# Another front for the first group of an RWKV-6 block: loads on two queues, norm and mixing shared between engines, and new due times

## The chip, the cores and the metric

The kernel runs on one core of one Trainium2 chip. The metric is device time in microseconds (us) of one launch. The engines carry these names: PE is TensorE (PEld its weight loads), DVE is VectorE, ACT is ScalarE, POOL is GpSimd, SP is SyncE, which here only issues DMAs. "SPq" and "ACTq" are the DMA-issuing sequencers of SP and ACT.

## The reference

One RWKV-6 block in f32 on x of 32 rows (batch) × 128 tokens × 512 channels; 32 heads of 16 channels. Cut to what matters:

```python
xn = ln(x, ln1_w, ln1_b); sx = shift(xn, prev) - xn       # shift: the token before, prev ahead of the first
xxx = tanh((xn + sx * maa_x) @ maa_w1)                    # 5 vectors of 32
xxx = matmul(xxx, maa_w2)                                 # 5 x 512
x5 = xn + sx * (maa_stack + xxx)                          # the five "mixings"
w = exp(-exp(time_decay + tanh(x5[1] @ decay_w1) @ decay_w2))
r, k, v = x5[3] @ Wr.T, x5[0] @ Wk.T, x5[2] @ Wv.T
g = silu(x5[4] @ Wg.T)
for t in tokens:                                          # per row and head, s is 16 x 16
    out[t] = r[t] . (u * k[t] v[t] + s)                   # the part with u is "the bonus"
    s = k[t] v[t] + w[t] * s
x = x + (group_norm(out) * gn_w + gn_b) * g @ Wo.T
xn2 = ln(x, ln2_w, ln2_b); sx2 = shift(xn2, prev) - xn2
x = x + sigmoid((xn2 + sx2*fr) @ Wr2.T) * (square(relu((xn2 + sx2*fk) @ Wk2.T)) @ Wv2.T)
```

## The kernel before

**Tiling.** The 32 rows are cut into eight groups of four (GB, NG). A group is N = 512 tokens, its 512 channels lie in NE = 4 chunks of 128 partitions, so that one tile is [128, 512] per chunk and one projection is 4 × 4 matmuls of 128×128 by 512 in f32 (`matmuls`, L392), each issued as two passes of PE.

**The front of a group.** `load_x` (L284) loads the four rows with tokens on partitions. `layernorm_T` (L320) takes the statistics on DVE (L333, L334), raises the variance to −1/2 on POOL (L353), normalises the rows on ACT (L358), transposes them on PE (L378) into a PSUM tile per chunk, and evicts each chunk with weight and bias to `xnT` on ACT (L368). `use` (L430) then writes the same affine form back into the PSUM tile (ACT, L434), takes the shift `sx` (DVE, L437) and the input `mx` of the first small matmul (DVE, L439). PE multiplies by maa_w1 (L445 and, through `first_split`, L398), ACT takes tanh (L449 to L454 and L405), and PE makes the five mixings' vectors in pairs of chunks (`side_by_side`, L411).

**Mixing.** `mixed` (L461) turns a pair into two chunks of x5. For most of them DVE multiplies in place in PSUM (L471) and adds xnT on its way to SBUF (L473). For groups after the first, the mixings 2, 3 and 4 (`ON_POOL`) have the product written to SBUF by DVE (L466) and the addition on POOL (L468). `front_proj` (L493) makes w (its tanh at L405, its exps at L514 and L516), then k, v and r for group 0 (k, r, v for the others); their results are put in lane order by DMAs that `to_lanes` issues (L421). `front_gate` (L547) makes g.

**The recurrence.** `prep` (L568) loads the state, folds two steps into one, and makes the bonus (`bonus`, L635 to L655: products of r and k, weighted with u). Each group has two halves of 17 units. A unit is a product of v and k on POOL (L705), a pair sum on POOL (L709), two copies on ACT (L680, L691), a scan on DVE (L727), a product with r on DVE (L729, tile `rm`), and eight accumulating matmuls on PE (L762, tile `acc`). The 17th unit of each half takes the bonus. `back` (L789) normalises by head, applies g, multiplies with Wo (L850) and does the feed-forward part (L924, L940).

**What sets the order.** The order of instructions on every engine is written out at build time. `Plan` holds streams (one generator per front, projection, recurrence part and so on), each with a due time that runs from a first to a last value (`DUE`, L49, in units of one group) as it advances. Of the streams whose next operation could start within `EPSILON` of the earliest by the planner's own costs, the one with the earliest due time goes first. So a new `DUE` table moves operations past one another on all engines, while dependencies stay. `warm` (L945) is such a stream: 180 transposes of the identity (L957) that nothing reads, spread over the first front where PE would be idle, and 120 near the end.

**Constants.** `constants` (L248) issues the loads of the small tensors: vec (all per-channel vectors), pv (the previous rows), maa_w1 (`w1_sb`), maa_w2 and decay_w2 (in halves on SP and ACT), decay_w1, and u in four pieces. Four small operations on POOL (L250 to L253) prepare the feed-forward vectors. `front_proj` of group 0 then loads Wv, Wk and Wr; `center` (L297) takes from Wv, on POOL, the mean over a head. Each DMA has a semaphore; eight of them are used in turn, so that a DMA waits for the one issued eight before it, whichever queue carried that.

**Buffers.** x, sc, a, rm and th have two, wt and mx three, blk four, xnT and sx one. PSUM has four tiles `ps`, two `sc` and one `acc`.

Of the kernel before, what the change touches and what calls it, by code (L numbers as in the profile page):

```python
# [11 lines left out]
ALU = mybir.AluOpType  # L12
# [7 lines left out]
GB = 4  # L20
# [24 lines left out]
ON_POOL = (2, 3, 4)  # L45
EPSILON = 0.0457


DUE = {"rec": (0.169, 1.075), "mix": (-5.141, -3.246), "proj": (-5.191, 5.259), "gate": (0.565, 0.599), "prep": (-4.508, 1.678), "back": (0.059, 3.118), "last1": (-21.936, 10.98), "warm0": (-5.0, -3.0), "warm1": (5.624, 7.819), "last2": (6.858, 12.052)}  # L49

# [132 lines left out]
def rwkv6_block(ctx: ExitStack, tc: tile.TileContext, x, prev, s0, vecs, u, maa_w1, maa_w2,  # L183
# [64 lines left out]
    def constants():  # L248
        nc.sync.dma_start(out=vec, in_=vecs)
        nc.gpsimd.tensor_scalar(ffn[:, 0, :], vec[:, V_FK, :], -1.0, 1.0, ALU.mult, ALU.add)  # L250
        nc.gpsimd.tensor_scalar(ffn[:, 2, :], vec[:, V_FR, :], -1.0, 1.0, ALU.mult, ALU.add)
        nc.gpsimd.tensor_tensor(ffn[:, 1, :], ffn[:, 0, :], vec[:, V_LN2B, :], ALU.mult)
        nc.gpsimd.tensor_tensor(ffn[:, 0, :], ffn[:, 0, :], vec[:, V_LN2W, :], ALU.mult)  # L253
        nc.sync.dma_start(out=pv, in_=prev)
        halves = lambda w, h: w.rearrange("r (f h p) -> h r f p", h=2, p=P)[h]
        nc.sync.dma_start(out=w1_sb, in_=maa_w1.rearrange("(c p) o -> p c o", p=P))
        for m in (1, 0, 2, 3, 4):
            for h, queue in enumerate((nc.sync, nc.scalar)):
                r = h * XD + (XM if m in (1, 3) else 0)
                queue.dma_start(out=w2p[r : r + XM, m, :].rearrange("r (f p) -> r f p", p=P),  # L260
                                in_=halves(maa_w2[m * XM : (m + 1) * XM, :], h))
            if m == 1:
                nc.sync.dma_start(out=dw1_sb, in_=decay_w1.rearrange("(c p) o -> p c o", p=P))
                for h, queue in enumerate((nc.sync, nc.scalar)):
                    queue.dma_start(out=dw2p[h * XD : (h + 1) * XD, :].rearrange("r (f p) -> r f p", p=P),
                                    in_=halves(decay_w2, h))
        for e in range(NE):
            nc.sync.dma_start(out=lanes(u_sb, e), in_=u[e * HE : (e + 1) * HE, :].unsqueeze(0).to_broadcast([GB, HE, S]))

    def lanes(t, e):  # L270


        return t[e::NE]
# [10 lines left out]
    def load_x(g, need=None, bs=range(GB)):  # L284
        b0, b1 = bs[0], bs[-1] + 1
        (xt,) = yield Op(SP, 0.4, w=[(0, None)], alloc=["x"], xfer=part(4.5, bs), need=need)
        nc.sync.dma_start(out=xt[:, b0:b1, :], in_=x[g * GB + b0 : g * GB + b1].rearrange("b t e -> t b e"))
        return xt
# [27 lines left out]
    def part(us, bs):  # L316

        return us if len(bs) == GB else us * len(bs) / GB + 0.03

    def layernorm_T(g, src, sums, vw, vb, which, use, take, need=None, bs=range(GB)):  # L320
# [34 lines left out]
        nc.vector.scalar_tensor_tensor(nb[:, bsl], mean, -1.0 if sums is None else 1.0, rstd[:, bsl], ALU.mult, ALU.mult)  # L355
        for b in bs:
            yield Op(ACT, 0.8, r=[(src, b), (nb, None), (rstd, None)], w=[(xh, b)])
            nc.scalar.activation(xh[:, b, :], src[:, b, :], AF.Identity, bias=nb[:, b : b + 1],  # L358
                                 scale=rstd[:, b : b + 1])
# [6 lines left out]
        def evict(e, pt):  # L366
            yield Op(ACT, part(0.78, bs), r=[(pt, None)], w=[(xnT, e)])
            nc.scalar.activation(xnT[:, e * GB + b0 : e * GB + b0 + nb_, 1 : L + 1], bt(pt[:, cols]), AF.Identity,  # L368
                                 bias=col(vb, e), scale=col(vw, e))
            yield from use(xnT, e, pt, tiles)  # L370
# [52 lines left out]
    def front_mix(g, d):  # L423

        xt = yield from load_x(g, (lambda: "x1" in data[g - 3]) if g > 2 else (lambda: "xin" in data[0]) if g else None)
        if g == 0:
            yield Op(SP, 5.5, xfer=4.0)
            yield Op(ACT, 3.9)
            constants()
        need = (lambda: "ln2" in data[g - 3]) if g > 2 else None  # L430
        def use(xnT, e, pt, tiles):
# [9 lines left out]
        xnT, sx, xin = yield from layernorm_T(g, xt, None, V_LN1W, V_LN1B, 0, use, ("sx", "mx"), need)  # L441
        d["xin"] = True
        (pm,) = yield Op(PE, 8 * PASS, r=[(xin, None)], w=[(0, None)], alloc=["ps"])
        for c in range(NE):
# [16 lines left out]
        def mixed(m, i, pp, x5):  # L461

            for f, p in zip((2 * i, 2 * i + 1), pp):
                if g and m in ON_POOL:
                    yield Op(DVE, 0.75, r=[(p, None), (sx, None)], w=[(x5, f)], end=[p])
# [27 lines left out]
    def front_proj(g, d):  # L493
# [4 lines left out]
        if g == 0:  # L498
            ws[2] = yield from weight(wv)
            plan.add(center(ws[2]), -1.0, -0.9, 8)  # L500
            ws[0] = yield from weight(wk)
            ws[3] = yield from weight(wr)
        yield Op(PE, 0.0, need=has(1))
        x5 = d["x5", 1]
# [63 lines left out]
    def prep(g, d):  # L568

        (st,) = yield Op(SP, 1.6, w=[(0, None)], alloc=["st"], xfer=1.5,  # L570
                         need=(lambda: "w01" in data[g - 1]) if g else None)
# [446 lines left out]
```

## Time and profile before

| | before |
|---|---|
| median of three runs | 1519.79 us (1518.50 to 1524.13) |
| the profiled execution itself | 1520.89 us |
| its span in the profile | 1519.1 us, so 1.8 us lie around it |
| mean granted PE clock | 0.969 |
| busy PE, DVE, POOL, ACT | 1433.7, 1266.1, 1026.1, 657.3 us |
| one group in the steady part | 170.4 us |

The profile gives busy time and share of each engine, then groups of instructions by line: operation, output and inputs, shape, count, busy time and mean in ns, and after the bar the idle time just before them and the instruction that ended it. In the timeline each row has its start and length in us, then engine, line, operation and the idle time before it with its releaser. The DMA-issuing rows (SPq, ACTq) show when a DMA was issued; when it landed is seen at the instruction that waited for it.

### The profile page before, as it was taken

How to read it: one execution, taken by the hardware profiler on the slowest of the kernel's cores; microseconds unless marked ns; L12 is line 12 of the kernel's file. 1: busy time of each engine (PE TensorE's matmuls, PEld its weight loads, DVE VectorE, ACT ScalarE, POOL GpSimd, SP SyncE). 2: the span in 40 equal slices, each digit the busy share in tenths (PEclk: the TensorE clock that was granted, in tenths of full speed). 3: DMA queues.
4: the chain of work that ended last, by engine and by line, in shares of the span. 5: the costliest groups of instructions: out<-in, count | busy, mean ns of one | idle time of the engine just before them, and what ended most of it. 6: DMA issues, size and time to landing. Idle time of an engine off the chain costs nothing.

```text
span 1519.1 us, 17193 instructions
## 1 busy us (share of the span) xinstructions
PE 1433.7 (94%) x5644; PEld 775.6 (51%) x5644; DVE 1266.1 (83%) x1618; ACT 657.3 (43%) x1279; POOL 1026.1 (68%) x632
## 2 busy tenths in 40 slices
PE   8997999899999999999999999999999999778998
PEld 7333454455544555455544555455544555454564
DVE  4537789989998899899988899899988888978742
ACT  4333243424743366423843365423833354344252
POOL 3014894877886959687786959687776959778500
PEclk9798999899999999999999999999999999889999
DMA  6120331334304521243304521344314421400220
GB/s 226 45 81 27 109 104 35 108 117 132 111 30 134 182 88 42 88 144 132 112 32 137 182 91 36 95 141 128 111 32 142 150 73 59 160 28 28 83 84 28
DMA packets 127561, 146.91 MB, mean 97 GB/s; under 512 B 8176, under 2 KB 77296, under 8 KB 126448
## 3 DMA queue, kind: packets, MB, share of 16 engines
q1 hardware_dynamic: 92112, 128.81, 25.5%
q10 hardware_dynamic: 35360, 17.02, 3.8%
q8 instruction: 44, 0.72, 0.2%
q14 instruction: 45, 0.37, 0.1%
HBM read 94.41 MB, written 17.83 MB: 74 GB/s over the span
## 4 chain that ended last, share of the span: by engine, by line
PE 50%; DVE 23%; POOL 14%; issue 6%; ACT 4%; DMA 2%; SPq 1%; ACTq 0%; POOLq 0%; DVEq 0%
PE ps L392 17%; POOL am L705 8%; PE acc L762 8%; PE ps L940 6%; PE ps L924 6%; PE ps L411 6%; POOL a L709 5%; DVE sc L727 4%; DVE rm L729 3%; PE ps L850 2%; PE ps L445 2%; DVE ps L635 2%; DMA x<-in_x 2%; PE ps L398 1%; DVE rk L643 1%
## 5 line engine op out<-in xcount | busy, mean ns | idle before, releaser
L705 POOL TENSOR_TENSOR am<-v,k 128x1024 f32<-128x1024 f32 x256 | 610.9, 2386 | 71.1 <-DMA r<-blk 52.7
L392 PE MATMUL ps<-mx,wt 128*128 128x512 f32 (+1 forms) x1312 | 581.3, 591 | 7.7 <-DVE mx L885 3.1
L709 POOL TENSOR_TENSOR a<-am 128x504 f32<-128x504 f32 x256 | 286.6, 1120 | 192.0 <-DVE sc L727 173.2
L392 PEld LDWEIGHTS ps<-mx,wt 128*128 128x128 f32 x1312 | 242.6, 193 | 273.7 <-issue 261.7
L729 DVE TENSOR_TENSOR rm<-sc,r 128x1024 f32<-128x1024 f32 x256 | 312.8, 1222 | 35.3 <-PE acc L762 20.3
L727 DVE TENSOR_TENSOR_SCAN sc<-sc,a 128x512 f32<-128x512 f32 x256 | 313.4, 1224 | 31.5 <-POOL a L709 28.7
L762 PE MATMUL acc<-by_head,rm 128*128 128x128 f32 x2176 | 288.6, 282 | 31.6 <-DVE rm L729 27.8
L762 PEld LDWEIGHTS acc<-by_head,rm 128*128 128x128 f32 x2176 | 250.9, 145 | 130.6 <-issue 56.5
L680 ACT COPY sc<-w 128x512 f32<-128x512 f32 x256 | 151.4, 592 | 230.4 <-DVE rm L729 200.5
L468 POOL TENSOR_TENSOR mx<-mx,xnT 128x512 f32<-128x512 f32 x84 | 99.5, 1196 | 40.0 <-DVE mx L466 39.4
L691 ACT COPY a<-st 128x8 f32<-128x8 f32 x256 | 51.4, 203 | 159.6 <-DVE sc L727 132.4
L924 PE MATMUL ps<-wt,mx 128*128 128x512 f32 x256 | 115.7, 594 | 0.0
L541 ACT COPY blk<-ps 128x512 f32<-128x512 f32 x96 | 56.0, 583 | 133.9 <-PE ps L392 127.4
L850 PE MATMUL ps<-wt,mx 128*128 128x512 f32 x256 | 111.7, 592 | 0.2 <-DVE rk L643 0.2
L353 POOL TENSOR_TENSOR rstd<-rstd,mhalf 128x4 f32<-128x4 f32 (+1 forms) x17 | 20.2, 1191 | 129.0 <-DVE rstd L351 129.0
L411 PE MATMUL ps<-tha,w2p 64*128 64x512 f32 x256 | 91.3, 676 | 14.3 <-DVE mx L473 6.8
L940 PE MATMUL ps<-wt,ev 128*128 128x512 f32 x224 | 101.7, 596 | 2.7 <-DVE mx L473 2.7
L471 DVE SCALAR_TENSOR_TENSOR ps<-ps,vec,sx 128x512 f32<-128x512 f32 x76 | 57.1, 752 | 34.7 <-PE ps L411 34.3
L466 DVE SCALAR_TENSOR_TENSOR mx<-ps,vec,sx 128x512 f32<-128x512 f32 x84 | 61.7, 743 | 22.1 <-PE ps L411 22.1
L850 PEld LDWEIGHTS ps<-wt,mx 128*128 128x128 f32 x256 | 48.2, 190 | 59.8 <-issue 55.0
L924 PEld LDWEIGHTS ps<-wt,mx 128*128 128x128 f32 x256 | 46.4, 190 | 51.1 <-issue 46.9
L940 PEld LDWEIGHTS ps<-wt,ev 128*128 128x128 f32 x224 | 40.5, 190 | 45.3 <-issue 39.7
(111 smaller groups left out, 1406.9 us busy)
## 6 DMA issues: line engine op xcount, KB each, us to landing
x<-in_x SPq DMA_DIRECT2D x15, 1024.0 KB
wt<-in_wk SPq DMA_DIRECT2D x8, 1024.0 KB
wt<-in_wr SPq DMA_DIRECT2D x8, 1024.0 KB
wt<-in_wg SPq DMA_DIRECT2D x8, 1024.0 KB
dgate<-blk SPq DMA_DIRECT2D x32, 256.0 KB
wt<-in_wo SPq DMA_DIRECT2D x8, 1024.0 KB
wt<-in_fk SPq DMA_DIRECT2D x8, 1024.0 KB
wt<-in_fr SPq DMA_DIRECT2D x8, 1024.0 KB
```

The source lines that it names most:

```text
L392: nc.tensor.matmul(p, lhsT=w[:, c, e * P : (e + 1) * P], rhs=xin[:, c, cols], start=(c == 0), stop=(c == NE - 1))
L411: nc.tensor.matmul(p.t, lhsT=w[h, :], rhs=t[h, :], start=True, stop=True)
L468: nc.gpsimd.tensor_tensor(bt(x5[:, f, :]), bt(x5[:, f, :]), row(xnT, f, 1), ALU.add)
L680: nc.scalar.copy(sc.t, d["w01"][:, q : q + 1, :].to_broadcast([P, DH, T2]))
L705: nc.gpsimd.tensor_tensor(am.t, v[:, ds, :], k[:, q : q + 1, :].to_broadcast([P, DH, L]), ALU.mult)
L709: nc.gpsimd.tensor_tensor(a[:, :, 1:T2], am2[:, :, 0 : T2 - 1, 0], am2[:, :, 0 : T2 - 1, 1], ALU.add)
L727: nc.vector.tensor_tensor_scan(scf, scf, a.t.rearrange("p d n -> p (d n)"), 0.0, ALU.mult, ALU.add)
L729: nc.vector.tensor_tensor(pair(rm.t), sc.t.unsqueeze(3).to_broadcast([P, DH, T2, 2]), r2[:, q : q + 1, :, :].to_broadcast([P, DH, T2, 2]), ...
L762: nc.tensor.matmul(acc[:, i, :], lhsT=rm[:, i, :], rhs=by_head, is_transpose=True, start=(q == 0 and i % 4 == 0), stop=(q == S), skip_grou ...
L850: nc.tensor.matmul(p.t, lhsT=att[:, c, b * L : (b + 1) * L], rhs=wot[:, c, :], start=(c == 0), stop=(c == NE - 1))
L924: nc.tensor.matmul(p.t, lhsT=xr[:, c, b * L : (b + 1) * L], rhs=frt[:, c, :], start=(c == 0), stop=(c == NE - 1))
L940: nc.tensor.matmul(p2.t, lhsT=kv[:, c, b * L : (b + 1) * L], rhs=fvt[:, c, :], start=(c == 0), stop=(c == NE - 1))
```

## The change

The loads of group 0: rows 0 and 1 are issued by SP, rows 2 and 3 by ACT, followed on ACT's queue by vec and pv, which leave the head of SP's. The four loads of u move from `constants` to `prep` of group 0, behind the three weights; the feed-forward vectors are made after the first front's `mx` (`of_norm2`). The norm of group 0: rows 1 and 3 on DVE, rows 0 and 2 on ACT. Its eviction from PSUM is on DVE instead of ACT. Its mixing: odd chunks take the form with POOL's addition (ten additions). `EPSILON` and all of `DUE` have new values, so the order of the other streams moves as well. The count of idle transposes (180 and 120) is the same. The lines of the changed kernel are up to 26 higher than those of before: L471 and L473 become L492 and L494, L466 and L468 become L487 and L489, L368's counterpart on DVE is L381, L434, L437 and L439 become L452, L455 and L457.

In the built programs, the order on PE is: 80 idle transposes, the transposes of chunks 0 and 1, 16 idle, chunk 2, 22 idle, chunk 3, 52 idle, the maa_w1 matmuls, 10 idle, then the pairs (before: 110, chunks 0 and 1, 18, chunk 2, 8, chunk 3, 28, maa_w1, 16). On DVE, per chunk of group 0: L381, L455, L457, one chunk after another; then the statistics of group 1, one L492, the statistics of group 2 (four rows), and the rest of the mixing. On SP: half of x, w1, the small weights, Wv, Wk, Wr, u in four, the state in four, then x of groups 1 and 2. In the recurrence of group 0 the scans stand ahead of most of the bonus; before, the bonus stood ahead of most scans. Before the end, 38 of the last idle transposes stand between the last accumulation and the last groups' transposes instead of 50, and the gates of both halves stand ahead of the first Wo matmul (L850).

```diff
@@ -43,10 +43,10 @@
 LANDING = 2.0
 HOP = (0.2, 0.05, 0.05, 0.04, 0.08)
 ON_POOL = (2, 3, 4)
-EPSILON = 0.0457
-
-
-DUE = {"rec": (0.169, 1.075), "mix": (-5.141, -3.246), "proj": (-5.191, 5.259), "gate": (0.565, 0.599), "prep": (-4.508, 1.678), "back": (0.059, 3.118), "last1": (-21.936, 10.98), "warm0": (-5.0, -3.0), "warm1": (5.624, 7.819), "last2": (6.858, 12.052)}
+EPSILON = 0.0395
+
+
+DUE = {"rec": (-0.253, 0.49), "mix": (-7.571, -5.137), "proj": (-8.154, 9.002), "gate": (-0.499, 0.231), "prep": (-5.528, 0.775), "back": (-1.364, 4.013), "last1": (-17.216, 13.228), "last2": (10.215, 24.226), "warm0": (1.568, 5.29), "warm1": (9.89, 17.928)}
 
 
 class Buf:
@@ -246,12 +246,6 @@
     nc.vector.memset(w2p, 0.0)
 
     def constants():
-        nc.sync.dma_start(out=vec, in_=vecs)
-        nc.gpsimd.tensor_scalar(ffn[:, 0, :], vec[:, V_FK, :], -1.0, 1.0, ALU.mult, ALU.add)
-        nc.gpsimd.tensor_scalar(ffn[:, 2, :], vec[:, V_FR, :], -1.0, 1.0, ALU.mult, ALU.add)
-        nc.gpsimd.tensor_tensor(ffn[:, 1, :], ffn[:, 0, :], vec[:, V_LN2B, :], ALU.mult)
-        nc.gpsimd.tensor_tensor(ffn[:, 0, :], ffn[:, 0, :], vec[:, V_LN2W, :], ALU.mult)
-        nc.sync.dma_start(out=pv, in_=prev)
         halves = lambda w, h: w.rearrange("r (f h p) -> h r f p", h=2, p=P)[h]
         nc.sync.dma_start(out=w1_sb, in_=maa_w1.rearrange("(c p) o -> p c o", p=P))
         for m in (1, 0, 2, 3, 4):
@@ -264,8 +258,12 @@
                 for h, queue in enumerate((nc.sync, nc.scalar)):
                     queue.dma_start(out=dw2p[h * XD : (h + 1) * XD, :].rearrange("r (f p) -> r f p", p=P),
                                     in_=halves(decay_w2, h))
-        for e in range(NE):
-            nc.sync.dma_start(out=lanes(u_sb, e), in_=u[e * HE : (e + 1) * HE, :].unsqueeze(0).to_broadcast([GB, HE, S]))
+
+    def of_norm2():
+        nc.gpsimd.tensor_scalar(ffn[:, 0, :], vec[:, V_FK, :], -1.0, 1.0, ALU.mult, ALU.add)
+        nc.gpsimd.tensor_scalar(ffn[:, 2, :], vec[:, V_FR, :], -1.0, 1.0, ALU.mult, ALU.add)
+        nc.gpsimd.tensor_tensor(ffn[:, 1, :], ffn[:, 0, :], vec[:, V_LN2B, :], ALU.mult)
+        nc.gpsimd.tensor_tensor(ffn[:, 0, :], ffn[:, 0, :], vec[:, V_LN2W, :], ALU.mult)
 
     def lanes(t, e):
 
@@ -283,6 +281,15 @@
 
     def load_x(g, need=None, bs=range(GB)):
         b0, b1 = bs[0], bs[-1] + 1
+        if g == 0:
+
+            (xt,) = yield Op(SP, 0.4, w=[(0, 0), (0, 1)], alloc=["x"], xfer=2.3)
+            nc.sync.dma_start(out=xt[:, 0:2, :], in_=x[0:2].rearrange("b t e -> t b e"))
+            yield Op(ACT, 1.4, w=[(xt, 2), (xt, 3)], xfer=2.3)
+            nc.scalar.dma_start(out=xt[:, 2:4, :], in_=x[2:4].rearrange("b t e -> t b e"))
+            nc.scalar.dma_start(out=vec, in_=vecs)
+            nc.scalar.dma_start(out=pv, in_=prev)
+            return xt
         (xt,) = yield Op(SP, 0.4, w=[(0, None)], alloc=["x"], xfer=part(4.5, bs), need=need)
         nc.sync.dma_start(out=xt[:, b0:b1, :], in_=x[g * GB + b0 : g * GB + b1].rearrange("b t e -> t b e"))
         return xt
@@ -354,6 +361,10 @@
         (nb,) = yield Op(DVE, 0.16, r=[(mv, None), (rstd, None)], w=[(0, None)], alloc=["nb"], port=True, end=[mv])
         nc.vector.scalar_tensor_tensor(nb[:, bsl], mean, -1.0 if sums is None else 1.0, rstd[:, bsl], ALU.mult, ALU.mult)
         for b in bs:
+            if g == 0 and sums is None and b % 2:
+                yield Op(DVE, 0.5, r=[(src, b), (nb, None), (rstd, None)], w=[(xh, b)], port=True)
+                nc.vector.tensor_scalar(xh[:, b, :], src[:, b, :], rstd[:, b : b + 1], nb[:, b : b + 1], ALU.mult, ALU.add)
+                continue
             yield Op(ACT, 0.8, r=[(src, b), (nb, None), (rstd, None)], w=[(xh, b)])
             nc.scalar.activation(xh[:, b, :], src[:, b, :], AF.Identity, bias=nb[:, b : b + 1],
                                  scale=rstd[:, b : b + 1])
@@ -364,9 +375,15 @@
         late = []
 
         def evict(e, pt):
-            yield Op(ACT, part(0.78, bs), r=[(pt, None)], w=[(xnT, e)])
-            nc.scalar.activation(xnT[:, e * GB + b0 : e * GB + b0 + nb_, 1 : L + 1], bt(pt[:, cols]), AF.Identity,
-                                 bias=col(vb, e), scale=col(vw, e))
+            if g == 0 and sums is None:
+
+                yield Op(DVE, 0.69, r=[(pt, None)], w=[(xnT, e)])
+                nc.vector.tensor_scalar(xnT[:, e * GB + b0 : e * GB + b0 + nb_, 1 : L + 1], bt(pt[:, cols]),
+                                        col(vw, e), col(vb, e), ALU.mult, ALU.add)
+            else:
+                yield Op(ACT, part(0.78, bs), r=[(pt, None)], w=[(xnT, e)])
+                nc.scalar.activation(xnT[:, e * GB + b0 : e * GB + b0 + nb_, 1 : L + 1], bt(pt[:, cols]), AF.Identity,
+                                     bias=col(vb, e), scale=col(vw, e))
             yield from use(xnT, e, pt, tiles)
 
         for e in range(NE):
@@ -424,9 +441,10 @@
 
         xt = yield from load_x(g, (lambda: "x1" in data[g - 3]) if g > 2 else (lambda: "xin" in data[0]) if g else None)
         if g == 0:
-            yield Op(SP, 5.5, xfer=4.0)
+            yield Op(SP, 5.0, xfer=4.0)
             yield Op(ACT, 3.9)
             constants()
+            d["constants"] = True
         need = (lambda: "ln2" in data[g - 3]) if g > 2 else None
         def use(xnT, e, pt, tiles):
 
@@ -440,6 +458,9 @@
 
         xnT, sx, xin = yield from layernorm_T(g, xt, None, V_LN1W, V_LN1B, 0, use, ("sx", "mx"), need)
         d["xin"] = True
+        if g == 0:
+            yield Op(POOL, 0.9)
+            of_norm2()
         (pm,) = yield Op(PE, 8 * PASS, r=[(xin, None)], w=[(0, None)], alloc=["ps"])
         for c in range(NE):
             nc.tensor.matmul(pm.t, lhsT=w1_sb[:, c, 0 : 4 * XM], rhs=xin[:, c, :], start=(c == 0), stop=(c == NE - 1))
@@ -461,7 +482,7 @@
         def mixed(m, i, pp, x5):
 
             for f, p in zip((2 * i, 2 * i + 1), pp):
-                if g and m in ON_POOL:
+                if m in ON_POOL if g else f % 2:
                     yield Op(DVE, 0.75, r=[(p, None), (sx, None)], w=[(x5, f)], end=[p])
                     nc.vector.scalar_tensor_tensor(x5[:, f, :], p.t, col(V_MAA + m, f), sx[:, f, :], ALU.add, ALU.mult)
                     yield Op(POOL, 1.08, r=[(xnT, None)], w=[(x5, f)], port=True)
@@ -496,10 +517,11 @@
         free = lambda: ("front", "weights") in data[g - 1]
         ws = {}
         if g == 0:
-            ws[2] = yield from weight(wv)
+            ws[2] = yield from weight(wv, lambda: "constants" in d)
             plan.add(center(ws[2]), -1.0, -0.9, 8)
             ws[0] = yield from weight(wk)
             ws[3] = yield from weight(wr)
+            d["weights"] = True
         yield Op(PE, 0.0, need=has(1))
         x5 = d["x5", 1]
         (pd,) = yield Op(PE, 2 * PAIR, r=[(x5, None)], w=[(0, None)], alloc=["ps"], end=[x5])
@@ -567,6 +589,10 @@
 
     def prep(g, d):
 
+        if g == 0:
+            yield Op(SP, 2.5, need=lambda: "weights" in d)
+            for e in range(NE):
+                nc.sync.dma_start(out=lanes(u_sb, e), in_=u[e * HE : (e + 1) * HE, :].unsqueeze(0).to_broadcast([GB, HE, S]))
         (st,) = yield Op(SP, 1.6, w=[(0, None)], alloc=["st"], xfer=1.5,
                          need=(lambda: "w01" in data[g - 1]) if g else None)
         s0g = s0[g * P : (g + 1) * P, :].rearrange("(b e h) k -> e b h k", e=NE, h=HE)
```

## Prediction

> **What bounds the kernel now.** I read the busy shares and slices first, then busy time by stretch, then the timeline of the first 60 us, then TensorE's (PE) and GpSimd's (POOL) own waits between 108 and 176 us.
>
> ```profile
> PE 1433.7 (94%) x5644; PEld 775.6 (51%) x5644; DVE 1266.1 (83%) x1618; ACT 657.3 (43%) x1279; POOL 1026.1 (68%) x632
> ...
> PEclk9798999899999999999999999999999999889999
> ```
>
> ```profile
> 120.00:140.00 20.00, 16.68 (x54) 7.16 (x50) 18.23 (x29) 6.65 (x16) 6.77 (x4) 0.85 0.02 5
> 140.00:160.00 20.00, 12.71 (x48) 6.47 (x47) 17.38 (x23) 7.92 (x17) 12.10 (x8) 0.72 0.09 26
> ...
> 260.00:280.00 20.00, 15.38 (x68) 9.76 (x69) 19.43 (x19) 8.66 (x21) 19.02 (x12) 0.85 0.04 16
> 280.00:300.00 20.00, 19.02 (x61) 9.20 (x60) 17.99 (x22) 8.07 (x13) 15.98 (x11) 0.81 0.44 134
> ...
> 474.67:645.03 170.36, 167.87 (x665) 88.70 (x665) 156.18 (x197) 80.59 (x156) 129.95 (x79) 1.00 0.33 106
> ```
>
> The columns after the stretch are its length, then busy PE, weight load, DVE, ACT, POOL, then PE's clock. A steady group takes 170.36 us with PE busy 167.87 (98.5%) at full clock: there only less PE work would help, and the change removes none. What can move lies before 300 us: at 120 to 160 PE is idle 10.6 us and its clock falls to 0.72, at 260 to 280 idle 4.6, and there DVE is the full engine (17.4 to 19.4 of 20). The work of the two programs stands in the same order from about 402 to 1070 us, bar a neighbouring swap per group, so whatever lead is won before 300 us is carried unchanged to the tail, where the order differs again.
>
> The first group's front:
>
> ```profile
> 11.04 2.93 ACT L358 ACTIVATE x<-x,nb,rstd 128x512 f32<-128x512 f32 x4 [2.95 <-DVE nb L355]
> ...
> 15.44 0.78 ACT L368 ACTIVATE xnT<-ps,vec 128x512 f32<-128x512 f32 x1 [1.35 <-PE ps L378]
> ...
> 16.25 0.75 ACT L434 ACTIVATE ps<-ps,vec 128x512 f32<-128x512 f32 x1
> 16.93 0.77 ACT L368 ACTIVATE xnT<-ps,vec 128x512 f32<-128x512 f32 x1
> 17.03 0.69 DVE L437 TENSOR_TENSOR sx<-xnT,ps 128x512 f32<-128x512 f32 x1 [6.02 <-ACT ps L434]
> ...
> 17.75 0.75 DVE L439 SCALAR_TENSOR_TENSOR mx<-sx,vec,ps 128x512 f32<-128x512 f32 x1
> ...
> 19.77 3.36 SPq L287 DMA_DIRECT2D x<-in_x  x2
> ...
> 22.44 3.60 PE L445 MATMUL ps<-mx,w_sb 128*128 128x512 f32 x8
> ...
> 30.91 0.69 DVE L333 BATCH_NORM_STATS2 stats<-x 128x6 f32<-128x512 f32 x1 [7.96 <-DMA x<-in_x]
> ...
> 34.31 0.75 DVE L471 SCALAR_TENSOR_TENSOR ps<-ps,vec,sx 128x512 f32<-128x512 f32 x1
> ...
> 35.10 0.69 DVE L473 TENSOR_TENSOR mx<-ps,xnT 128x512 f32<-128x512 f32 x1
> ```
>
> ACT takes 1.49 us per chunk (L368 and L434) with DVE beside it. DVE then idles 7.96 us for group 1's rows, whose statistics stand ahead of the first mixing, which starts at 34.31 although its matmul began at 29.72. The first scan comes late too:
>
> ```profile
> 132.71 1.03 POOL L709 TENSOR_TENSOR a<-am 128x504 f32<-128x504 f32 x1 [15.00 <-DVE sc L727]
> ```
>
> ```profile
> 148.94 2.04 PE L411 MATMUL ps<-tha,w2p 64*128 64x512 f32 x2 [3.13 <-DVE a L655]
> ```
>
> POOL waits 15.00 us because the bonus (L635 to L655, about 12 us) is ahead of the scans on DVE.
>
> **What the Trainium skill says.** "DMA: Bandwidth & Descriptors", "Issuing engines are not separate DMA queues": transfers issued by different engines run on the same 16 DMA engines, so two queues save issue time only. Here one issue of x takes 0.45 us, so I give two queues nothing. "PSUM — Partial Sum Buffer", "The four PSUM rules": POOL cannot touch PSUM. The trace agrees as far as it goes: every POOL addition (L468, 1.196 us) reads SBUF and follows a DVE L466 that has moved the product there. "VectorE: DVE Perf Modes", "Mode 2×_2P": an f32 tensor_scalar from SBUF may run at two elements a cycle, from PSUM not; no row of before shows the former, and 0.69 to 0.75 fits one element a cycle from PSUM. "TensorE: Matmul & The Clock Gate", "What's actually happening": an idle window of about 3.4 us drops the clock; 0.72 at 140 to 160 agrees, so a closed gap returns cold time too.
>
> **The change, step by step.** Durations are from the profiled execution: span 1519.1, itself 1520.89; the three runs have median 1519.79, 1.1 lower.
>
> Load. x of group 0 lands at about 6.2 either way (first statistics 6.21): 0. Bounds: 1 us earlier if both halves stream faster, 1 later if vec and pv push in. The vectors come before the evict at 12.7 with room. Moving vec, pv and u off the head of SP's queue lets wv, wk and wr issue at about 10 to 12 us (before 15.5 to 17.0). But the DMAs' semaphores rotate over eight, each DMA waiting for the one eight earlier: before, w1 waited till 7.33 so. In the new order the state loads wait for the three weights, and group 1's x, queued behind them, issues at about 21.8 instead of 19.77. It lands at about 27 (before 30.9), as the traffic is over sooner.
>
> Norm. Two of four rows stay on ACT, 2×0.80 = 1.6 instead of 2.93, two go to DVE: −1.4. One on DVE costs between 0.35 (from the skill's double rate) and 0.69 (L437); either fits beside ACT's 1.6. Transposes start at 12.65 instead of 14.69, since 80 idle transposes stand ahead instead of 110 (13.62/110 = 0.124 each, done by 11.3): −2.0.
>
> Evict, moved to DVE. Per chunk DVE's new order is evict, sx, mx, with ACT's L434 between: 0.69+0.75+0.69+0.75, with hops 2.97, a chain, against 1.49. Four: 11.9 from 13.4, so mx is complete at 25.3, before 22.94: +2.4. Tanh follows at 29.1 and the first pair at about 32.05 (29.72). Here the change loses.
>
> Statistics. Group 1's rows land at 27, so their 3.3 us lie in 27.1 to 30.4, hidden under the tanh chain: first mixing 32.6, −1.7 against 34.31. The cover is worth up to 3.3 if x lands later than 29.3, each further us costing one.
>
> Mixing. Odd chunks: DVE L466 0.743 and POOL L468 1.196 instead of L471 0.752 and L473 0.69. DVE pays 0.75+0.69+0.74 = 2.2 a pair, not 2.88; four masks have eight pairs: −5.4. Group 2's statistics (3.4, ahead of most of the mixing now, interleaved before) do not change the sum. POOL has nothing else to do then. But the chain mixing 1, w's tanh and exps stands behind the late first pair and ACT's eight norms of groups 1 and 2; I walk it to k's projection at 57.1, before 60.05: −3.0, with bounds −5 and −1. v's projection gains 0.7 more, as its slot is freed by one 0.75 instead of 1.48. Everything up to the copy of r: −3.7.
>
> First scans. The new order puts scans ahead of the bonus: first scan at about 120.3 (131.34), so POOL's wait goes; k of group 1 about 162 (174.35). The bonus is still owed. DVE's rows from r's copy to group 1's first scan sum to 163.95 us, before 164.7, which from 120.39 to 297.96 left 12.9 idle. Lead = 297.96 − (116.7 + 163.95 + idle) = 17.3 − idle. Least idle is the 2.4 at its start, which gives 14.9; as before, 12.9, gives 4.4. I take the middle, 7.65: lead 9.65. PE does not take it away: k starts 12 early. But near the end of group 0's first half DVE, with 38.2 us of rows since 159.9, is the late one, and PE idles about 8.5 there.
>
> Tail. 38 idle transposes instead of 50 save 0.6 (taken as a piece of what follows); both halves' gates are now ahead of the first Wo matmul (L850), about 3.0 later, of which the chain behind gives back 0.8 and more: +1.5, bounds −1 and +3.
>
> Sum: 1520.89 − 9.65 + 1.5 = 1512.7; less 1.1 for the median, **1511.6 us**.
>
> **Rivals.** First, the whole lead: DVE idles 2.4 only, the PE holes at 260 to 300 close too and the tail costs nothing: 1520.89 − 14.9 − 1.1 = 1505. For it: POOL's 15 us wait and 10.6 us of idle PE are plain. Against: DVE at 19.4 of 20 at 260 to 280 has no slack to sell.
>
> Second, the front's gain is lost or only carried: 12.9 us of DVE idle as before leaves 4.4, tail +1.5 or +3: 1517 to 1518.4; with the front's 3.7 lost as well, 1522. For it: the evict chain is twice as long, and the work on DVE is the same within 0.7 us.
>
> Third, slower: the deferred bonus. Its 12 us of DVE fall where PE has only the accumulations and one projection left, DVE waits unit by unit for POOL's 2.39 and 1.12 us (L705, L709), and PE waits for rm at each half's end. Price: idle beyond 17.3 us is a loss; with the tail's 1.5 the time passes 1527.4 from 23 us of idle DVE between r's copy and group 1's first scan. At 25 it is 1520.89 + 7.7 + 1.5 − 1.1 = 1529. Against: before had 12.9 with a plainer stall.
>
> **How the numbers follow.** 0.5% (7.6 us) is about what a measurement of this kernel can tell from no change; faster then means below 1512.2. Main case 0.42 (half below that), whole lead 0.22, front lost 0.24, slower 0.12. Faster 0.21+0.22 = 0.43; same 0.21+0.24 = 0.45; slower 0.12. The main case's own range is 1508 to 1515 (idle 4 to 11). The whole range: 1503.5 (lead 14.9, tail −1, median) to 1522.
>
> **What would show it.** In the trace of after: last mx chunk of group 0 near 25.3; first mixing near 32.6 with group 1's statistics over; k at 57; first scan near 120 and no 15 us wait on POOL; k of group 1 near 162; PE waiting for rm near 198; group 1's first scan near 288; a steady group still 170.4. A steady group that differs, or x of group 1 after 29, makes the prediction wrong.

## The result, and the profile after

| | before | after |
|---|---|---|
| median | 1519.88 us (six runs, 1518.05 to 1524.13) | 1528.10 us (six runs, 1525.79 to 1531.74) |
| ratio, 95% interval | | 1.0053 [1.0035, 1.0071] |
| the profiled execution, its span | 1520.89, 1519.1 | 1531.74, 1529.9 |

The forecast was 1511.6; the kernel became 8.2 us slower. The two profiled executions lie 10.8 us apart, more than the medians, as that of the changed kernel is the slowest of its six. A single trace is good to about 2 us: e7, e11, e14 and e17 below have the changed kernel's order of instructions up to the first scan, and reach it at 115.2 to 117.5, the changed kernel at 117.6. The front of group 0, in the timeline of the changed kernel:

```profile
11.08 1.52 ACT L369 ACTIVATE x<-x,nb,rstd 128x512 f32<-128x512 f32 x2
...
13.13 0.81 DVE L381 TENSOR_SCALAR xnT<-ps,vec 128x512 f32<-128x512 f32 x1 [1.73 <-PE ps L395]
...
24.51 0.75 DVE L457 SCALAR_TENSOR_TENSOR mx<-sx,vec,ps 128x512 f32<-128x512 f32 x1
...
28.80 0.69 DVE L340 BATCH_NORM_STATS2 stats<-x 128x6 f32<-128x512 f32 x1 [3.54 <-DMA x<-in_x]
...
32.20 0.75 DVE L492 SCALAR_TENSOR_TENSOR ps<-ps,vec,sx 128x512 f32<-128x512 f32 x1
```

```profile
56.62 3.70 PE L409 MATMUL ps<-mx,wt 128*128 128x512 f32 x8 [1.38 <-DVE mx L494]
```

```profile
113.00 1.23 DVE L617 TENSOR_TENSOR r<-r,w 128x1024 f32<-128x1024 f32 x1 [6.21 <-DMA st<-in_s]
117.56 1.23 DVE L753 TENSOR_TENSOR_SCAN sc<-sc,a 128x512 f32<-128x512 f32 x1 [3.33 <-ACT a L717]
```

mx is complete at 25.26, the first mixing begins at 32.20, k's projection at 56.62, r's copy at 113.00 and the first scan at 117.56: at or ahead of the forecast's 25.3, 32.6, 57.1, 116.7 and 120.3. The gain is there, and is 13.8 us at the first scan (131.34 before). Then it is lost. Busy time by stretch, of the changed kernel (columns as in the forecast; behind PE's clock stand the DMA engines' busy share and GB/s):

```profile
140.00:160.00 20.00, 12.75 (x38) 6.80 (x36) 15.65 (x21) 7.28 (x15) 16.05 (x9) 0.54 0.43 134
...
180.00:200.00 20.00, 13.07 (x41) 7.62 (x42) 16.44 (x17) 2.79 (x7) 17.12 (x11) 0.74 0.01 4
...
260.00:280.00 20.00, 10.91 (x41) 4.34 (x39) 19.27 (x31) 3.04 (x7) 4.31 (x2) 0.78 0.00 0
280.00:300.00 20.00, 19.29 (x46) 7.76 (x46) 12.91 (x17) 6.72 (x12) 6.47 (x4) 0.71 0.55 173
```

```profile
486.95:657.31 170.36, 167.74 (x666) 88.71 (x664) 156.19 (x197) 80.50 (x156) 129.82 (x79) 1.00 0.32 106
```

The kernel before, for comparison:

```profile
180.00:200.00 20.00, 20.00 (x86) 10.98 (x85) 15.15 (x16) 7.09 (x17) 19.30 (x13) 1.00 0.27 80
```

PE idles 6.9 us at 180 to 200, where before it idled not at all, and 9.1 at 260 to 280, where before it was 4.6. A steady group is 170.36 us as before, so the loss is made before the steady part. The start of every 16th scan (L727, then L753), read from the DVE timeline, measures where; a half of a group has 16 scans:

| scan | before | after | what it opens |
|---|---|---|---|
| 0 | 131.34 | 117.56 | group 0, first half |
| 16 | 212.26 | 206.50 | group 0, second half |
| 32 | 297.88 | 302.22 | group 1, first half |
| 48 | 390.57 | 404.86 | group 1, second half |
| 64 | 462.69 | 475.29 | group 2 |
| 255 (last) | 1426.60 | 1439.05 | |

The lead of 13.8 us is 5.8 at scan 16, gone at 32 (4.3 late), and 14.3 late at 48. From 64 on the distance stays at 12.6 and 12.5; the tail gives 1.7 back (spans 10.8 apart).

### The profile page after: what moved, and what is told of

Its sections match the earlier page's. It is cut to its first block, busy times and chain, and to the rows that moved or that the text cites. A ratio compares the mean times of both kernels' runs of the same rounds, so it can differ in the third digit from the quotient of the medians.

```text
span 1529.9 us, 17203 instructions
## 1 busy us (share of the span) xinstructions
PE 1428.6 (93%) x5644; PEld 776.3 (51%) x5644; DVE 1273.9 (83%) x1614; ACT 652.6 (43%) x1273; POOL 1038.9 (68%) x642
## 5 line engine op out<-in xcount | busy, mean ns | idle before, releaser
L735 POOL TENSOR_TENSOR a<-am 128x504 f32<-128x504 f32 x256 | 287.6, 1123 | 181.4 <-DVE sc L753 164.8
L753 DVE TENSOR_TENSOR_SCAN sc<-sc,a 128x512 f32<-128x512 f32 x256 | 313.2, 1224 | 35.0 <-POOL a L735 30.2
L489 POOL TENSOR_TENSOR mx<-mx,xnT 128x512 f32<-128x512 f32 x94 | 111.8, 1200 | 84.7 <-DVE mx L487 84.1
L876 PE MATMUL ps<-wt,mx 128*128 128x512 f32 x256 | 111.2, 592 | 0.0
L360 POOL TENSOR_TENSOR rstd<-rstd,mhalf 128x4 f32<-128x4 f32 (+1 forms) x17 | 20.6, 1212 | 122.2 <-DVE rstd L358 122.2
L428 PE MATMUL ps<-tha,w2p 64*128 64x512 f32 x256 | 83.2, 680 | 16.0 <-DVE mx L494 8.3
L487 DVE SCALAR_TENSOR_TENSOR mx<-ps,vec,sx 128x512 f32<-128x512 f32 x94 | 69.1, 742 | 22.4 <-PE ps L428 22.3
L492 DVE SCALAR_TENSOR_TENSOR ps<-ps,vec,sx 128x512 f32<-128x512 f32 x66 | 49.7, 753 | 37.4 <-PE ps L428 36.8
L876 PEld LDWEIGHTS ps<-wt,mx 128*128 128x128 f32 x256 | 48.5, 190 | 60.3 <-issue 56.7
```

The source lines that it names most:

```text
L428: nc.tensor.matmul(p.t, lhsT=w[h, :], rhs=t[h, :], start=True, stop=True)
L489: nc.gpsimd.tensor_tensor(bt(x5[:, f, :]), bt(x5[:, f, :]), row(xnT, f, 1), ALU.add)
L735: nc.gpsimd.tensor_tensor(a[:, :, 1:T2], am2[:, :, 0 : T2 - 1, 0], am2[:, :, 0 : T2 - 1, 1], ALU.add)
L753: nc.vector.tensor_tensor_scan(scf, scf, a.t.rearrange("p d n -> p (d n)"), 0.0, ALU.mult, ALU.add)
L876: nc.tensor.matmul(p.t, lhsT=att[:, c, b * L : (b + 1) * L], rhs=wot[:, c, :], start=(c == 0), stop=(c == NE - 1))
```

## The experiments

There are two theories. Theory A: the new order costs the time, and the front's edits gain. Theory B: the front's edits themselves cost (the chain on DVE, the additions on POOL). Within A, the cost can lie in the deferred bonus (the third case of the forecast) or in something else in the order. Each ratio below is to the kernel before, with its 95% interval.

**Exchanging the due times.** Three kernels plan anew:

```diff
 # e1_front_only, on the changed kernel: both lines as before
-EPSILON = 0.0395
+EPSILON = 0.0457
 # e2_due_only: the reverse, the new DUE and EPSILON on the kernel before
 # e3_rec_due, on the changed kernel
-"rec": (-0.253, 0.49)
+"rec": (0.169, 1.075)
```

> The changed kernel with DUE and EPSILON of the kernel before: loads, norm, eviction, mixing and the place of u stay as changed, the order is made anew from the old due times. Theory A (the new order, which puts group 0's recurrence ahead of the next fronts, costs the time; the front's edits gain): 1513 to 1519 us, and TensorE's time lost to idling and cold clock up to 480 us near 57 to 60 us, against 62 before and 83 after. Theory B (the edits of the front themselves cost, by the longer chain on DVE and the additions on POOL): 1524 to 1531.

> The kernel before with DUE and EPSILON of the changed one, no edit of the front. Theory A: 1525 to 1536, slower than the kernel before by 5 or more, as the order alone carries the loss. Theory B: 1515 to 1522.

> The changed kernel with only the recurrence's due times as before, (0.169, 1.075) instead of (-0.253, 0.49); all other due times and EPSILON as changed. If the lead given to the recurrence over the fronts is what costs (A1): 1513 to 1521, and group 0's units 20 to 30 no longer 20 to 28 us ahead of before. If another part of the table or the front costs: 1524 to 1532.

Measured: 1615.80 us (1.0629 [1.0602, 1.0656]), 1617.90 (1.0641 [1.0615, 1.0667]) and 1580.40 (1.0397 [1.0372, 1.0422]). All three missed every range. With a due table that was not made for its operations, the planner decides otherwise in every group, also in the steady part that was not to move: in e1, PE's busy time at 1000 to 1100 falls to 87 us (98 before). These runs say nothing on A or B; the order has to be held fixed.

```diff
 # e4_bonus_first, on the changed kernel, planned anew
-plan.add(first_bonus(d, k, r), 0.0, 0.4, 27)
+plan.add(first_bonus(d, k, r), -0.6, -0.2, 27)
```

> The changed kernel with the due times of group 0's first bonus moved from 0.0 to 0.4 to -0.6 to -0.2, so that it stands ahead of the scans again. If the deferred bonus is what costs (the third case of the forecast, A2): 1513 to 1521, no TensorE idling of 7 us between 180 and 200. If the loss lies at the change from group 0 to group 1 and in group 1: 1523 to 1531, with the idling at 180 to 200 gone and that at 260 to 280 and 340 to 350 kept.

1520.36 us (1.0007 [0.9995, 1.0018]): no change from the kernel before, and 7.7 below the changed kernel. It would speak for the deferred bonus, but the rest of the plan is another too (scan 24 at 254.35, not at 233.17). e8 below decides.

**The order held fixed.** From here on a kernel carries the list of choices that a planner made, and replays it:

```diff
-            t, st = self.pick(best)
+            key, n = KEYS[raw[at]], raw[at + 1]
...
+            st = next(x for x in self.streams if x[5] == key)
 # e5_front_old_order: the changed kernel, the list of the kernel before
 # e6_old_front_new_order: the kernel before, the list of the changed kernel
```

> All edits of the first front as changed, but every stream is taken in the very order in which the planner of the kernel before took them (the list of its choices is written into the kernel and replayed; the three operations that only the changed kernel has go where their stream stands). TensorE's order is that of before to the instruction. Theory A (the new order costs, the front's edits gain 2 to 6 us): 1514 to 1518 us. Theory B (the front's edits cost): 1522 to 1531.

> The front of the kernel before, with the choices of the changed kernel's planner replayed; TensorE's order is that of the changed kernel to the instruction. Theory A: 1529 to 1535, the new order's loss without the front's gain. Theory B: 1516 to 1522.

1516.74 us (0.9981 [0.9974, 0.9988]) and 1537.42 (1.0111 [1.0095, 1.0126]). This shows theory A, and B falls: the edits alone gain 3.3 us, and the new order alone costs 17.4. The two do not simply add: both together are 8.2 late, so in the new order the edits are worth 9.3. e5's scan 0 is at 123.94, scan 32 at 291.83, scan 64 at 456.69: its lead of 6 us at 32 stays. Beside e5, which has the same front, the changed kernel starts its scans 6.4 us earlier and is level at scan 16 (206.50, e5 206.55); at 32 it is 10.4 us behind, at 48 20.3.

**Pieces of the change inside the new order.**

```diff
 # e7_no_reload: load_x(..., first=False)
-        if g == 0:
+        if first:
 # e8_bonus_local: in the list of the changed kernel, the 24 choices of first_bonus:
 #   20 ahead of the first scan's, 4 ahead of the 13th choice of rec_dve
 # e13_g1_mix_on_dve
-                if m in ON_POOL if g else f % 2:
+                if m in ON_POOL if g > 1 else f % 2 and not g:
 # e14_back_early: in the list, choices 2 to 9 of back(0) 13 choices of rec_dve earlier
```

> The changed kernel, its order replayed, without one thing that I had overlooked: load_x is also called for the residual of group 0, near 362 us, and there loads x in two halves and vec and pv a second time on ACT's queue; here the residual takes the plain load. If the second load of vec and pv stalls their readers: 1523 to 1526. If it costs nothing that can be measured: 1527 to 1529.

1530.24 us (1.0070 [1.0057, 1.0083]): no gain. In the changed kernel `load_x` also serves the residual of group 0, and so loads vec and pv a second time, which the forecast had missed; that is not the cause.

> The changed kernel, its order replayed, with one piece moved by hand: group 0's bonus goes to just ahead of the first scan (its products with u) and to before the fifth unit (the rest), instead of among units 6 to 17. Nothing else is moved. If the deferred bonus costs by itself: 1517 to 1523, no idling of 7 us at 180 to 200. If the earlier result of a replanned bonus came from the rest of the new plan: 1526 to 1531.

1529.80 us (1.0064 [1.0052, 1.0076]). The deferred bonus is not the cause. Busy time by stretch of e8, where it is out of the way:

```profile
140.00:160.00 20.00, 13.23 (x61) 8.25 (x58) 18.06 (x18) 8.61 (x18) 15.10 (x10) 0.83 0.17 53
160.00:180.00 20.00, 16.77 (x44) 7.55 (x44) 14.25 (x16) 3.95 (x11) 17.80 (x13) 0.74 0.40 139
180.00:200.00 20.00, 15.07 (x65) 9.92 (x62) 12.24 (x12) 3.90 (x10) 19.36 (x13) 0.74 0.07 20
```

PE still idles 14.9 us in these 60 (15.4 in the changed kernel), and now DVE idles as well, 7.8 at 180 to 200, where POOL is the full engine. Scan 16 is at 206.91, in the changed kernel at 206.50.

> The changed kernel, its order replayed, with group 1's mixing additions (twelve of L489, 1.17 us each) on DVE in the form of L492 and L494 instead of POOL. Theory F (POOL is the full engine at 166 to 200, where its additions for group 1 stand between the sums of group 0's units, and PE and DVE wait for it): 1519 to 1525 us, PE's idling of 7 us at 180 to 200 down to 3 or less. Theory G (DVE is the bound there too, and gets 8 us more work): 1528 to 1536.

1531.53 us (1.0069 [1.0053, 1.0085]), inside the range of theory G. PE still idles 6.1 us at 180 to 200, where theory F asked for 3 or less. So POOL's additions are not the bound alone either: what is taken off POOL lands on DVE (17.8 busy there, 16.4 in the changed kernel), and nothing is won.

> The changed kernel, its order replayed, with the norm by head of group 0 (the chain of nine 128x128 operations and the product on y) moved ahead on DVE to the unit where it stood before, some 13 choices of the recurrence earlier. In the changed kernel it runs beside POOL's products and takes 11.7 us instead of 3, and PE then waits 5.66 us for it. If that wait is a loss of its own: 1518 to 1523. If the time is lost again to the next late thing: 1525 to 1530.

1542.72 us (1.0137 [1.0120, 1.0155]), above both ranges. DVE stands still in this kernel's timeline:

```profile
362.26 0.69 DVE L941 SCALAR_TENSOR_TENSOR mx<-ps,blk 128x512 f32<-128x512 f32 x1 [14.48 <-DMA blk<-dgate]
```

The loads of the gates are on SP's queue behind others, and only DVE was moved. What a hand-moved step waits for on another queue has to be moved with it; so the run doesn't tell what PE's wait of 5.66 us for this norm (shown under "The port") is worth.

**Which groups of choices.**

```diff
 # e9_rec_placed_old: recurrence placed by the old list, all else in the new list's order
 # e10_rec_placed_new: the reverse
 # e11_new_to_half0, e17_new_to_half1: new list to the last unit of group 0's
 #   first half (second half), then the old list's choices that are left
 # e15_old_to_half0: old list to there, then the new
```

> The changed kernel with all streams but the recurrence's in the new order among themselves, and each operation of the recurrence placed after as many other operations as in the order of before. Theory C (what costs is that the recurrence of group 0 was pulled ahead of the next groups' fronts): 1515 to 1520 us. Theory D (what costs is the order of fronts, bonus, gate and back among themselves): 1525 to 1531.

> The reverse: the front's edits, all streams but the recurrence's in the order of before among themselves, and the recurrence placed among them as in the changed kernel. Theory C: 1525 to 1533. Theory D: 1515 to 1520.

1577.26 us (1.0379 [1.0361, 1.0396]) and 1564.61 (1.0293 [1.0279, 1.0307]): both far outside, so neither C nor D. Both mixtures of the recurrence's places and the rest's order cost more than either order.

> The changed kernel in its new order up to the last unit of group 0's first half (206 us in its trace), then, of what is left, in the order of before. If the loss is made by then (TensorE lost 14 us more than before between 140 and 220): 1525 to 1530. If it is made later, at 260 to 290 and 340 to 350: 1515 to 1520. In between, both have a part.

> The front's edits in the order of before up to the last unit of group 0's first half, then, of what is left, in the new order; the reverse of the run that changed over there (1525.0, against 1516.7 for the old order throughout and 1528.1 for the new). If the two parts add up, 1528.1 - 8.3 = 1519.8: 1518 to 1522. If the loss after that point needs what came before it: 1515 to 1518.

> The changed kernel in its new order up to the last unit of group 0 (near 300 us), then in the order of before. With the change-over at 206 us it was 1525.0, with none 1528.1. If the second part of the loss is made by the end of group 0 (PE's idling at 260 to 290): 1527 to 1530. If it is made in group 1 (336 to 360): 1523 to 1526.

1525.04 us (1.0034 [1.0021, 1.0048]), 1529.07 (1.0051 [1.0037, 1.0065]) and 1529.06 (1.0046 [1.0028, 1.0065]). By their medians alone the three contradict one another: e11 puts most of the loss ahead of the end of the first half, e15 behind it. The scans show more than the medians (us from one to the next, order in force in brackets):

| scans | before | e5 (old) | after (new) | e11 | e15 | e17 |
|---|---|---|---|---|---|---|
| 0 to 16 | 80.9 | 82.6 | 88.9 | 95.4 (new) | 80.4 (old) | 88.9 (new) |
| 16 to 32 | 85.6 | 85.3 | 95.7 | 87.0 (old) | 91.9 (new) | 99.3 (new) |
| 32 to 48 | 92.7 | 92.7 | 102.6 | 92.8 (old) | 101.6 (new) | 95.9 (old) |
| 48 to 64 | 72.1 | 72.2 | 70.4 | 72.2 (old) | 70.4 (new) | 72.1 (old) |

Each half takes about as long as the order in force there gives it: with the new order the first half of group 0 is 6 to 8 us longer, the second 6 to 10, the first of group 1 9 to 10, and the fourth 2 shorter. In the first half that is only the earlier start of the scans not being kept, as scan 16 is where e5 has it. But other work is owed there: by scan 16 the profile has 677 matmuls on PE in the changed kernel and 700 in e5. Where the order changes back to the old one, such work is done first, and the stretch up to the change grows (e11's 95.4, e17's 99.3): e11 has 695 matmuls by scan 16, and is 6.4 us behind e5. So the medians don't add: 1516.74 + 8.3 + 12.3 would be 1537.3, the changed kernel has 1528.1. The expected 1518 to 1522 for e15 took e11's 8.3 for a cost of the first half, and was wrong for that reason.

**The port.** e12 measures by itself what stretches DVE's operations beside POOL:

```diff
+    vector()                        # 12 each: L206, L208, L210, L212
...
+    for _ in range(30):
+        nc.gpsimd.tensor_tensor(pb, pa, pa, ALU.mult)
...
+    vector()
```

> Not the block: only runs of twelve DVE operations each (f32 tensor_tensor 128x128 and 128x512 with both inputs in SBUF, scalar_tensor_tensor 128x512 in place in PSUM with one input in SBUF, tensor_scalar 128x512 from SBUF), first alone, then beside a row of POOL products of 128x1024; the output holds none of the block. If a DVE operation with two inputs in SBUF has to wait until POOL's running instruction ends: 0.29 and 0.68 us alone, and beside POOL about 2.4 us for the mean of each, while the form in PSUM stays at 0.75. If the two share the port turn by turn: at most twice as long, 0.6 and 1.4.

Its timeline (one execution), first alone, then beside POOL:

```profile
4.18 3.88 DVE L206 TENSOR_TENSOR s<-s,xb 128x128 f32<-128x128 f32 x12 [2.02 <-DMA xb<-in_x]
7.98 8.68 DVE L208 TENSOR_TENSOR t<-xa,xb 128x512 f32<-128x512 f32 x12
16.57 9.49 DVE L210 SCALAR_TENSOR_TENSOR ps<-ps,c,xb 128x512 f32<-128x512 f32 x12
...
34.22 63.80 POOL L218 TENSOR_TENSOR pb<-pa 128x1024 f32<-128x1024 f32 x30
34.79 23.65 DVE L206 TENSOR_TENSOR s<-s,xb 128x128 f32<-128x128 f32 x12
58.36 25.96 DVE L208 TENSOR_TENSOR t<-xa,xb 128x512 f32<-128x512 f32 x12
84.25 9.48 DVE L210 SCALAR_TENSOR_TENSOR ps<-ps,c,xb 128x512 f32<-128x512 f32 x12
```

The 128x128 product goes from 0.32 (3.88/12) to 1.97 us, the 128x512 one from 0.72 to 2.16, about one POOL product each (POOL's take 1.89 and 2.22 in the two stretches); the form with one input in PSUM stays at 0.79. So a DVE operation with both inputs in SBUF waits for POOL's running instruction, one for one, as the first case expected. The Trainium skill says this in "SBUF — State Buffer", "SBUF: two separate sides": the shared pair of ports "is an exclusive lock, not a bandwidth split"; for DVE the run agrees. POOL is hardly held up in turn: 1.89 us beside the small product, as beside the form in PSUM, and 2.22 beside the large one. In the changed kernel the norm by head of group 0 falls beside POOL's products; the kernel before first, then the changed one:

```profile
313.48 2.40 DVE L812 TENSOR_SCALAR th<-th 128x128 int32<-128x128 int32 x1
315.91 0.29 DVE L815 TENSOR_TENSOR th<-th 128x128 f32<-128x128 f32 x1
316.24 0.29 DVE L816 SCALAR_TENSOR_TENSOR th<-th 128x128 f32<-128x128 f32 x1
316.57 0.29 DVE L817 SCALAR_TENSOR_TENSOR th<-th 128x128 f32<-128x128 f32 x1
```

```profile
335.98 1.09 DVE L841 TENSOR_TENSOR th<-th 128x128 f32<-128x128 f32 x1
337.10 1.07 DVE L842 SCALAR_TENSOR_TENSOR th<-th 128x128 f32<-128x128 f32 x1
338.20 2.39 DVE L843 SCALAR_TENSOR_TENSOR th<-th 128x128 f32<-128x128 f32 x1
```

```profile
347.80 1.97 PE L856 MATMUL ps<-ident,y 128*128 128x128 f32 x8 [5.66 <-DVE y L845]
```

The nine operations from L841 on take 9.4 us instead of 2.9, and PE waits 5.66 for what they end in. That the stretch is real is shown; how much of the 10 us of that half it makes is not. The chain grew by 6.5, but the three steps ahead of it (L810 to L812) were stretched in the kernel before, 4.2 us against 1.8 in the changed one, so over the whole norm DVE pays about 4.1 us more.

**What of the front gains.** Both in the order of before:

```diff
 # e16_old_order_act_evict: the eviction of group 0 back on ACT
-            if g == 0 and sums is None:
+            if False:
 # e18_no_pool_adds: that, and the additions back on DVE
-                if m in ON_POOL if g else f % 2:
+                if m in ON_POOL and g:
```

> The front's edits in the order of before, with the eviction of group 0's rows back on ACT. If the chain of four operations a chunk on DVE costs on the path: mx complete about 5 us earlier than 28.7, the first mixing then bound by group 1's statistics at about 33.1 instead of 34.75, so 1514 to 1516, below 1516.7. If it costs nothing: 1516 to 1518.

> As the kernel with the order of before and the eviction back on ACT (1514.5), now also with group 0's additions back on DVE; what is left of the edits are the loads and the norm. The forecast's step: two pairs of chunks in eight cost DVE 2.88 instead of 2.2 each, 5.4 us in all, of which 3 reach k's projection. If so: 1517 to 1519. If the loads and the norm bring the gain and the additions nothing: 1514 to 1516.

1514.52 us (0.9965 [0.9952, 0.9978]) and 1518.73 (0.9990 [0.9975, 1.0004]). e16 beats both kernels and has the lowest median here. Its interval touches that of e5, and its last scan is only 0.4 us earlier (1421.19, 1421.59), so what the eviction on DVE costs is not settled beyond that it gains nothing. The additions on POOL are what gains: scan 0 moves from 127.77 (e18) to 123.61 (e16) with them, the median by 4.2. Loads and norm alone (e18) can't be told from no change in the median.

## Why the prediction was wrong

- **Load, norm, transposes, evict, statistics, mixing: right, and in part too small.** mx, the first mixing and k's projection came within 0.5 us of the forecast. Group 1's x was issued at 23.33 instead of 21.8, and its statistics began at 28.8 instead of 27.1. The first pair's matmul was done at 31.81 and the first mixing began at 32.20, when the statistics were over, so the late x cost 0.4 us at most. r's copy gained 7.4, not 3.7. k's projection had gained 3.4; of the other 4.0, 2.8 come from the first 32 matmuls of the projection, which took 14.00 us at full clock instead of 16.78 at 0.83. The forecast counted no clock there. The two rows of the norm on DVE took 0.50 each, between the bounds; the evict 0.81 instead of 0.69.
- **POOL's wait was to go, and did not.** Instead of one wait of 15.00 us for the first scan, POOL waits 7.83 and 5.39 for the first two (L735, until 118.93 and 127.79). The other signs of the first half came: k of group 1 at 164.09 (forecast 162), and PE waiting for rm, 7.6 us in three waits between 179 and 190 (forecast 8.5 near 198).
- **First scans: this step failed.** It is "Lead = 17.3 − idle", with idle put at the middle of 2.4 and 12.9. By the durations of the rows, DVE's work from r's copy to group 1's first scan is 168.7 us (165.8 before, by the same sum), and idle, which is what is left, is 20.6 (11.7 before). With r's copy at 113.0 that gives 113.0 + 168.7 + 20.6 = 302.3, against 297.9 before: 4.4 late. Against the forecast's 288.3, idle is 13.0 over, the rows 4.7 over, and r's copy 3.7 ahead. The rows should have shrunk by 0.75 and grew by 2.9 (the products of the bonus, L661 and L674, took 16.5 us instead of 10.1, beside POOL; other rows shrank). The idle was the larger error: its upper bound was "as before", with no reason why a new order couldn't idle more. Rows overlap a little; the profile's own sums of DVE's busy time, before and after, give the same picture:

```profile
120.39:297.88 177.49, 156.39 (x586) 79.15 (x583) 156.29 (x192) 63.71 (x135) 126.94 (x78) 0.91 0.21 66
112.93:302.22 189.29, 160.71 (x588) 82.39 (x585) 159.34 (x190) 64.44 (x137) 126.75 (x77) 0.84 0.23 74
```

- **What DVE waited for in that time.** Its named waits behind r's copy are 26.4 us, 17.7 before. Those for PE fell from 16.0 to 12.4; those for ACT and POOL rose from 1.7 to 14.0, the longest, at 292.80, is 5.15 at a gate (L586, waiting for ACT's tanh, L584).
- **The third case ended on the right side, by another way, which is luck.** Its mechanism, the deferred bonus, falls with e8. Its threshold, idle of 23 us, was not reached: 20.6 and the longer rows made 4.4 us by group 1's first scan. The rest of the loss came behind it, where no case of the forecast looked. In place of the mechanism the runs show a loss of the new order in two halves: against the same front in the old order (e5), none by scan 16, 10.4 us by scan 32, 20.3 by scan 48.
- **What happens there, as far as it is shown.** Group 0's second half runs ahead (scan 24 at 233.17 instead of 261.22), and then DVE has group 1's mixing, bonus and foldings in one piece, 258 to 280: DVE 19.27 busy, PE 10.91 and POOL 4.31. POOL stands still for most of it, until DVE has folded group 1's k:

```profile
275.61 3.20 POOL L731 TENSOR_TENSOR am<-v,k 128x1024 f32<-128x1024 f32 x1 [18.93 <-DVE k L630]
```

Scan 31 comes 26.8 us after scan 30, before 7.8. The lead in the recurrence was borrowed from the next group's front. For the half before, the trace names PE waiting for DVE and DVE for POOL in turn, and neither moving the bonus (e8) nor taking additions off POOL (e13) helps; a single cause there stays open.
- **After group 1's first scan: the second step that failed.** "Whatever lead is won before 300 us is carried unchanged" counted nothing between 300 us and 402, where the orders meet. 10 us more were lost there, in scans 32 to 48 (102.6 us instead of 92.7), with the stretched norm among them; what makes up the rest is open. That the orders meet at 402 us bounds the loss in time, not in size.
- **Tail: +1.5 expected, −1.7 measured** (12.45 late at the last scan, 10.8 at the end). The first Wo matmul of the tail (L876) is at 1463.44, 12.6 behind the kernel before, as the last scan is: the gates ahead of it cost nothing.
- **Sums of the forecast that don't come out.** The rows before are 165.8 us with 11.7 idle, not 164.7 with 12.9, and the lower end of the whole range works out at 1503.9, not 1503.5. Neither changes the outcome.
- **Overlooked:** the second use of load_x, which e7 shows to cost nothing.

## What to carry to other kernels

When a change moves both operations and the order of everything around them, hold the order fixed and exchange one of the two; here the plan's parameters exchanged alone gave 4 to 6% of loss and said nothing. An early start of a chain is worth something only if the work that it overtakes isn't due at the chain's end: before counting the lead, follow it to the same point one group further. And ask of each DVE operation with two SBUF inputs what POOL will be doing beside it after the move.

## What was not expected of the hardware

The wait at the port is one POOL instruction per DVE operation with two SBUF inputs, also for a short one: 0.32 becomes 1.97 us for a 128x128 product, six times as long. A scalar_tensor_tensor that reads one input from PSUM is not touched (0.79 in both). A tensor_scalar from SBUF, 0.58 alone (0.55 median), took up to 2.00 in the part that still ran beside POOL, so one tensor input from SBUF can wait too.
